# How four tiles of the first layernorm are turned, and how every turned tile is moved, in a hybrid attention block

## The chip, the cores and the metric

The kernel runs on one core of one Trainium2 chip. The metric is the device time of one execution in microseconds; it is given as the median of several runs. One execution is also recorded by the hardware profiler; its span and its rows are what the text calls the profile and the trace.

## The reference, cut to what matters

The input x is 2 x 1024 x 512 in fp32. Four blocks follow each other, each on the layernorm of the running x, and each added to it.

```python
x = x + attn_a(layernorm(x), ...)   # chunks of 128: gated linear attention with decay
x = x + ffn(layernorm(x), ...)      # silu(x Wg) * (x Wu), then Wd; integer weights, hidden 1408
x = x + attn_b(layernorm(x), ...)   # softmax attention over 1024 positions, output weights
x = x + ffn(layernorm(x), ...)      # the same ffn again

def layernorm(x, eps=1e-5):
    m = mean(x, -1); v = var(x, -1)
    return (x - m) / sqrt(v + eps)

# attn_a, for one chunk of 128 tokens and one head of 128:
# q, k, v = projections (k normalised); alpha = sigmoid, beta = softplus of projections
# cla = cumsum(log(alpha + 1e-6)); decay = exp(cla_i - cla_j), causal
# y = (q k^T * beta * decay) v + (q state) * exp(cla)
# state = state * exp(cla_end) + v^T (k * beta * exp(cla_end - cla))
```

Every projection contracts over the 512 features. TensorE contracts over partitions, so a normed tile, which has tokens on partitions, must be turned until it has features on partitions.

## The kernel before, in words

**Tiles and groups.** The 2048 tokens are 16 tiles of 128; four tiles are a group (`ST = 4`). The normed x of a group, turned, is called xT (128 partitions by 4 x 512). The four norms are named a (input of attn_a), f (first ffn), b (attn_b) and g (second ffn); x1, x2 and x3 are the running x after the first, second and third block, kept in DRAM as 16 tiles each.

**Precision.** Products that need fp32 are made of three fp32r products (`mm3`, L89 to L91): each operand is split into a high part (ScalarE cast, L75) and a low part (subtraction on VectorE, L76).

**Two ways of turning.** For the first two groups of norm a (tiles 0 to 7), `ln_tile` normalises a tile on VectorE (xn, L122) and `layernorm_T` transposes its four 128 x 128 pieces on TensorE (L130) into PSUM, from which the split is made. All other groups, 14 in number, go through `ln_steps`: four norm steps (`ln_norm`: load x at L102, statistics at L109 and L111, three small GpSimd operations, xn, then one VectorE transpose of 32 x 32 blocks into the tile y, L198) and four moves (`ln_move`, L209: four transfers each, from 32 partitions of y to 32 partitions of xT, with the blocks of 32 tokens interleaved, so that one piece is 32 values or 128 bytes). `ln_split` then splits xT.

**Order.** An ordered list of Python calls says what each engine does next, and a scheduler orders instructions by it. `behind(...)` adds edges: what is written in it comes after the given instructions. In attn_a, the start is: the product M of two weights, tiles 0 to 3, gate projections, then for each head i `q_head(0, i)`, with tiles 4 to 7 between them, then the loads and splits of Wk and Wv (`load_wqkv`, `load_wv`), the keys and values of tile 0 (`kv_tile(0)`), and a loop over the 16 tiles. In turn t of the loop stand the query projections of head t of the next group (`q_head`), the keys and values of tile t + 1, the scores of tile t, and the steps in `fill[t]`, which hold norm steps of later groups. `spill` writes M to DRAM: `m_d`, L181 and L183.

**Queues.** The loads of x and weights, the stores and most xT transfers are issued in order by SyncE (SP). Some xT transfers of norms b and g go by GpSimd.

**The late operand step.** In the second half of attn_b, `combine("g", 0)` prepares the second ffn's operands from xT in a list of steps called `moving`. `do(moving, n)` runs the next n. One of them, T1, is a subtraction (L257), a ScalarE cast and a VectorE subtraction of 128 x 1024.

The names that the text uses: pWk and pWv are the products for keys and values, pq those for queries, pS the scores' product, pob the output product of attn_b with ptl and pth the split probabilities; `lu` and `la` are the logs of the gates, for which ScalarE loads a function table.

Of the kernel before, what the change touches and what calls it, by code (L numbers as in the profile page):

```python
# [9 lines left out]
F32 = mybir.dt.float32  # L10
# [6 lines left out]
P = 128  # L17
# [8 lines left out]
ST = 4  # L26
# [8 lines left out]
def hybrid_block_kernel(ctx: ExitStack, tc: tile.TileContext, a, out):  # L35
# [30 lines left out]
    def behind(inss):  # L66

        es = ExitStack()
        for ins in inss:
            es.enter_context(tc.issue_after(ins))  # L70
        return es
# [28 lines left out]
    def load_x(src, name, tag="xin"):  # L100
        xin = (rp if tag == "xres" else xp).tile([P, D], F32, tag=tag, name=f"xin_{name}")
        nc.sync.dma_start(out=xin, in_=src)  # L102
        return xin
# [31 lines left out]

    bq_s, sg_s, su_s = cols[:, 0:H], cols[:, H : H + KH], cols[:, H + KH : H + 2 * KH]

    x_in = a["x"]
    x1 = [dp.tile([P, D], F32, tag=f"x1_{t}", name=f"x1_{t}") for t in range(NT)]
    x2 = [dp.tile([P, D], F32, tag=f"x2_{t}", name=f"x2_{t}") for t in range(NT)]  # L140
    x3 = [dp.tile([P, D], F32, tag=f"x3_{t}", name=f"x3_{t}") for t in range(NT)]
    cl_d = [dp.tile([16, P], F32, tag=f"cl_{g}", name=f"cl_{g}") for g in range(NST)]
    p_d = [dp.tile([T // P, P, P], F32, tag=f"p_{i}", name=f"p_{i}") for i in range(NC)]
    vo_d = [dp.tile([P, 1024], F32, tag=f"vo_{k}", name=f"vo_{k}") for k in range(KD)]
# [43 lines left out]
    def ln_norm(src, nm, st, i):  # L188


        t = st * ST + i
        for n in range(t, min(t + 2, st * ST + ST)):
            if (nm, n) not in lnX:
                lnX[nm, n] = load_x(src[n], f"{nm}{n}")
        if i == 0:
            lnY[nm, st] = yp.tile([P, 4, KD, ST, 32], F32, tag="y", name=f"y_{nm}{st}")
        xn = layernorm(lnX[nm, t], f"{nm}{t}", by_act=nm in "af")
        done = nc.vector.transpose(lnY[nm, st][:, :, :, i, :], xn.rearrange("p (k b q) -> p b k q", k=KD, b=4))  # L198
        laid[:] = [done.ins]

    def ln_move(nm, st, b):

        if b == 0:
            lnT[nm, st] = slot(f"xT_{nm}{st}").rearrange("p (k c) -> p k c", k=KD)
        y = lnY[nm, st]
        xf = lnT[nm, st].bitcast(F32).rearrange("p k (i b q) -> p (k i) b q", i=ST, b=4)
        for c in range(4):
            sync = nm in "af" or (nm, st) in (("b", 0), ("b", 1), ("g", 3)) or ((nm, st) == ("b", 2) and c % 2)
            (nc.sync if sync else nc.gpsimd).dma_start(  # L209
                out=xf[32 * b : 32 * (b + 1), :, c, :],  # L210
                in_=y[32 * c : 32 * (c + 1), b].rearrange("p k i q -> p (k i) q"),
            )

    def ln_split(nm, st):
# [133 lines left out]
    with ExitStack() as actx:  # L348
# [41 lines left out]
        def load_wv():  # L390
            wv = slot("Wv")
            wqkv["Wv"] = [wv[:, k * 512 : (k + 1) * 512] for k in range(KD)]
            for k in range(KD):
                w = wqkv["Wv"][k]
                stg = sp.tile([P, 512], F32, tag="stg", name=f"stg_Wv{k}")
                nc.sync.dma_start(out=stg[:, 0:256], in_=a["Wv"][k * P : (k + 1) * P, 0:256])
                with behind(normed_x):
                    split(w[:, 0:256], w[:, 256:512], stg[:, 0:256], nc.gpsimd if k % 2 else None)

        def load_wqkv(nm, staged=None):  # L400
# [8 lines left out]
                    done.extend(split(w[:, 0:512], w[:, 512:1024], staged[:, k]))  # L409
            return load if staged is None else done  # L410

        xa = [x_in[t * P : (t + 1) * P, :] for t in range(NT)]

        def ln_tile(t):
            st, i = divmod(t, ST)
# [4 lines left out]

        def sm(shape, nm, st, dt=F32):
            return a3.tile([P] + shape, dt, tag=nm, name=f"{nm}_{st}")

        vbs = []

# [151 lines left out]
        def kv_tile(t):  # L577
            kv_part(t, "Wk")
            kv_part(t, "Wv")
# [133 lines left out]
        with behind((end,)):  # L713
            gate_proj(0)
        load_wqkv("Wq", staged)
        for i in range(4):
            ends.clear()
            q_head(0, i)
            with behind((wq_loaded, *ends.values())):
                for t in ((), (4,), (5,), (6, 7))[i]:  # L720
                    ln_tile(t)
            if i == 0:
                load_wqkv("Wk")
            if i == 1:
                with behind((*normed_x, *copied)):
                    spill(ap, ("kT", "kw", "sdec", "at"), pm, m_d, "M")
        load_wv()
        kv_tile(0)
        decays(0)
        k_norm(0)  # L730

        fill = [[] for _ in range(NT)]
        for src, nm, g, its in (
            (xa, "a", 2, (0, 0, 0, 1, 1, 1, 1, 1)),
            (xa, "a", 3, (2, 2, 3, 4, 4, 5, 5, 5)),
            (x1, "f", 0, (6, 6, 7, 7, 7, 7, 8, 8)),
            (x1, "f", 1, (9, 9, 10, 10, 10, 10, 11, 11)),
        ):
            for t, step in zip(its, ln_steps(src, nm, g)):
                fill[t].append(step)  # L740

        def a_split(g):
            for step in ln_split("a", g):
                step()
            xTa[g] = lnT["a", g]

        moving = combine("f", 0)
        wcs, loads = [], []
        for t in range(NT):
            if t + 4 < NT:  # L750
                q_head(*divmod(t + 4, ST))
            if t == 0:
                decay_rows(0)
                load_row(0)
                load_row(1)
            load_row(t + 1)
            if t + 1 < NT:
                kv_tile(t + 1)
            weighed = scores(t)
            if t % ST == 0 and t + ST < NT:  # L760
                gate_proj(t // ST + 1)
            if t + 1 < NT:
                with behind((*(normed[t + 1][2:] or normed[t][2:]), *key_copy)):
                    decay(t + 1)
            if t == NT - 2:
                with behind(key_copy):
                    for n in (1, 2):
                        loads.append(product_operands(sp, a["WvT"], a["Wo"], "V", n))
                with behind(parts[-4:]):
                    late_norm.pop()()  # L770
            if t in (3, 7):
                with behind(key_copy):
                    a_split(t // 4 + 2)
            with behind(normed.get(t + 1, (weighed,))):
                for step in fill[t]:
                    step()
                if 1 <= t <= KH:
                    down_weights(sp, t - 1)
                for n in {NT - 3: (0,), NT - 1: (3,)}.get(t, ()):
                    loads.append(product_operands(sp, a["WvT"], a["Wo"], "V", n))  # L780
                if t == NT - 3:
                    first_codes = [
                        load_codes(xp, "xn", a["wgu"][0][:, n * 512 : (n + 1) * 512], f"cf0_{n}") for n in range(2)
                    ]
                if t == NT - 2:
                    wcs.append(stationary(0, "f0", loaded=first_codes))

                    room = staging("codes").bitcast(I32)
                    for j in (2, 3):
                        held[j] = [room[:, 2 * j - 4 + n] for n in range(2)]  # L790
                        for n in range(2):
                            nc.sync.dma_start(out=held[j][n], in_=a["wgu"][j][:, n * 512 : (n + 1) * 512])
                for n in range(3 if NT - 4 <= t < NT - 1 else 0):
                    moving.pop(0)()
                if t == NT - 1:
                    wcs.append(stationary(1, "f0", (sp, "stg")))
            if (t + 2) % ST:
                load_row(t + 2)
            if t == NT - 2:
                prep = weight_product(loads, "V")  # L800
            if t >= NT - 2:
                next(prep)
# [5 lines left out]
    def ffn(src, dst, nm, wcs, moving, ended, after):  # L808
# [3 lines left out]
        with ExitStack() as fctx:  # L812
# [5 lines left out]
            for pr in range(2):  # L818
# [90 lines left out]
                for i in range(2 * ST):  # L909
# [4 lines left out]
                            done = h_split(n, js, ha[:, n - 2, js] if n < ST else hb[:, n - ST, js], None)  # L914
                    xr = rp.tile([P, D], F32, tag="xres", name=f"xr{nm}{t}")
                    with behind((half,)):
                        nc.sync.dma_start(out=xr, in_=src[t])
                    o = fp.tile([P, 512], F32, tag="sg", name=f"o{nm}{t}")

                    last = nm == "g" and t == NT - 1  # L920
# [17 lines left out]

    of_b = combine("b", 0)
    ffn(  # L940
        x1,
        x2,
        "f",
        wcs,
        moving,
        spilled,
        (ln_steps(x2, "b", 0) + ln_steps(x2, "b", 1), of_b[:6]),
    )


# [2 lines left out]
    with ExitStack() as bctx:  # L953
# [209 lines left out]
        def do(steps, n):  # L1163
            with behind(last):
                for _ in range(n):
                    steps.pop(0)()
# [32 lines left out]
        wvo = blocks(vo_d, "wvo0_")  # L1199
        moving = of_b[6:]  # L1200
        for b in range(NB):
            nm, src, g = ("b", x2, 2) if b == 0 else ("g", x3, 0)
            norm = ln_steps(src, nm, g) + ln_steps(src, nm, g + 1)
            if b == 0:
                for kt in (4, 5, 6, 7):
# [49 lines left out]
            def between():  # L1255
                out_b(b, 3)
                if b:
                    with behind(summed):
                        do(moving, 2)

            cycle(b, 3, between)
            if b == 0:
# [5 lines left out]
        probs_T(1, 7)  # L1268
        probs_split(1, 7, last)
        with behind(splits):  # L1270
            do(moving, 6)
        array(out_b, 1, 5)
        array(out_b, 1, 6)
        wcs = [stationary(n, "g0") for n in range(2)]
        ended = (array(out_b, 1, 7),)

    out_t = [out[t * P : (t + 1) * P, :] for t in range(NT)]
    ffn(x3, out_t, "g", wcs, moving, ended, ([], []))


# [60 lines left out]
```

## Time and profile before

| | us |
|---|---|
| median of 3 runs | 927.32 |
| lowest and highest | 926.01, 927.61 |
| the profiled execution's own time | 926.9 |
| span of its trace | 925.2 |
| TensorE busy | 918.5 |
| VectorE busy | 690.4 |
| ScalarE busy | 433.9 |
| GpSimd busy | 257.4 |

The profiled execution's own time is 1.7 us above its span, which runs from the first to the last recorded instruction. TensorE was granted its full clock on average (1.0). Busy times overlap, so they aren't added up: what counts is which engine is on the chain that ended last, and what that engine waited for. A row of a transfer gives its count, its size and the median time from issue to landing; an engine's row gives the count, and the duration of one.

### The profile page before, as it was taken

The numbers are of one execution on the slowest core, as the hardware profiler recorded it, in microseconds if no ns is written. First come the engines' busy times: TensorE is split into PE (matmuls) and PEld (weight loads), VectorE is DVE, ScalarE is ACT, GpSimd is POOL, SyncE is SP. The second block draws the span as 40 slices with busy tenths as digits, with TensorE's granted clock in tenths as the row PEclk, the third lists the DMA queues.
The fourth block names the chain that finished last, engine by engine and source line by source line (L and its number), as shares of the span: only waits on it lengthen the run. The fifth ranks groups of instructions, "written<-read, shape, count | busy, mean of one in ns | idle before, by whom it ended". The sixth has DMA issues, their size and how long they took to land.

```text
span 925.2 us, 13659 instructions
## 1 busy us (share of the span) xinstructions
PE 918.5 (99%) x4546; PEld 778.1 (84%) x4546; DVE 690.4 (75%) x1335; ACT 433.9 (47%) x928; POOL 257.4 (28%) x458
## 2 busy tenths in 40 slices
PE   9999999999999999999999999999999999999998
PEld 7899999998888888888888888888878888888887
DVE  6755657479998798778848878569968886967654
ACT  5645365556776334444234444145434444344431
POOL 4345334557563002211130401140501631001100
PEclk9999999999999999999999999999999999999999
DMA  9535655477979754724733769225969735454022
GB/s 304 210 100 124 208 160 152 158 207 262 367 236 321 214 178 153 216 47 150 281 82 83 171 168 261 69 45 137 239 140 369 259 126 137 165 205 138 22 69 80
DMA packets 216182, 162.20 MB, mean 175 GB/s; under 512 B 151024, under 2 KB 167728, under 8 KB 216112
## 3 DMA queue, kind: packets, MB, share of 16 engines
q1 hardware_dynamic: 212624, 150.05, 53.7%
q0 software_dynamic: 3488, 11.28, 4.5%
q8 instruction: 36, 0.59, 0.3%
q14 instruction: 34, 0.28, 0.1%
HBM read 104.76 MB, written 41.84 MB: 158 GB/s over the span
## 4 chain that ended last, share of the span: by engine, by line
PE 94%; DVE 2%; SPq 1%; DMA 1%; issue 1%; ACT 0%; POOL 0%; DVEq 0%; ACTq 0%
PE pXf L338 4%; PE pog L925 4%; PE pog L924 4%; PE pZf L338 4%; PE pof L925 4%; PE pXg L338 4%; PE pVg L338 4%; PE pVf L338 4%; PE pZg L338 4%; PE pof L924 4%; PE pob L91 3%; PE pob L89 3%; PE pob L90 3%; PE psZ L1023 2%; PE psX L1023 2%; PE psV L1023 2%
## 5 line engine op out<-in xcount | busy, mean ns | idle before, releaser
L924 PE MATMUL pog<-wdg,hsg 128*128 128x512 f32 (+1 forms) x165 | 60.1, 375 | 0.0
L925 PE MATMUL pog<-wdg,hsg 128*128 128x512 f32 (+1 forms) x165 | 60.0, 375 | 0.0
L925 PE MATMUL pof<-wdf,hsf 128*128 128x512 f32 x154 | 59.1, 389 | 0.0
L924 PE MATMUL pof<-wdf,hsf 128*128 128x512 f32 x154 | 58.9, 389 | 0.0
L91 PE MATMUL pob<-vh,ptl 128*128 128x512 f32 x128 | 49.9, 390 | 0.8 <-DVE ptl L76 0.8
L89 PE MATMUL pob<-vh,pth 128*128 128x512 f32 x128 | 49.9, 390 | 0.0
L90 PE MATMUL pob<-vl,pth 128*128 128x512 f32 x128 | 49.8, 389 | 0.0
L76 POOL TENSOR_TENSOR hsg<-sgg,hsg 128x128 fp32r<-128x128 f32 x40 | 18.9, 491 | 110.4 <-ACT hsg L75 102.6
L338 PE MATMUL pXg<-B_g,wcg 128*128 128x512 f32 x176 | 46.2, 389 | 0.0
L338 PE MATMUL pVf<-T_f,wcf 128*128 128x512 f32 x176 | 46.2, 389 | 0.0
L338 PE MATMUL pVg<-T_g,wcg 128*128 128x512 f32 x176 | 46.2, 389 | 0.0
L338 PE MATMUL pXf<-B_f,wcf 128*128 128x512 f32 x176 | 45.9, 390 | 0.0
L113 POOL TENSOR_SCALAR ve_g<-mv_g 128x1 f32<-128x1 f32 x16 | 7.7, 486 | 129.6 <-DVE mv_g L111 129.6
L209 POOL DMA_DIRECT2D xT_g<-y_g x48 | 31.1, 655 | 38.5 <-DVE T_b L76 29.2
L338 PEld LDWEIGHTS pXf<-B_f,wcf 128*128 128x128 f32 x176 | 32.9, 188 | 7.1 <-issue 0.3
L338 PEld LDWEIGHTS pVf<-T_f,wcf 128*128 128x128 f32 x176 | 33.0, 188 | 6.9
L338 PEld LDWEIGHTS pVg<-T_g,wcg 128*128 128x128 f32 x176 | 33.0, 188 | 6.9
L338 PEld LDWEIGHTS pXg<-B_g,wcg 128*128 128x128 f32 x176 | 33.0, 188 | 6.9
L545 ACT ACTIVATE row<-row,ncl 128x128 f32<-128x128 f32 x64 | 20.5, 391 | 35.4 <-POOL row L534 35.4
L113 POOL TENSOR_SCALAR ve_b<-mv_b 128x1 f32<-128x1 f32 x16 | 5.7, 359 | 112.4 <-DVE mv_b L111 112.2
L924 PEld LDWEIGHTS pog<-wdg,hsg 128*128 128x128 f32 x165 | 31.1, 188 | 5.7
L925 PEld LDWEIGHTS pog<-wdg,hsg 128*128 128x128 f32 x165 | 31.0, 188 | 5.6
(344 smaller groups left out, 2837.4 us busy)
## 6 DMA issues: line engine op xcount, KB each, us to landing
wcg<-wc SPq DMA_DIRECT2D x19, 896.0 KB, 5.0
wc<-wcf SPq DMA_DIRECT2D x11, 896.0 KB, 5.8
p<-py SPq DMA_DIRECT2D x15, 512.0 KB, 3.5
wcf<-wc SPq DMA_DIRECT2D x8, 896.0 KB, 6.3
ptl<-p SPq DMA_DIRECT2D x56, 128.0 KB, 3.1
xin_a<-in_x SPq DMA_DIRECT2D x16, 256.0 KB, 5.3
xra<-in_x SPq DMA_DIRECT2D x16, 256.0 KB, 3.4
row<-cl SPq DMA_DIRECT2D x16, 256.0 KB, 4.3
```

The source lines that it names most:

```text
L76: return c.ins, (eng or nc.vector).tensor_tensor(lo, src, hi.bitcast(F32), ALU.subtract).ins
L89: nc.tensor.matmul(ps, lhs_hi, rhs_hi, start=first, stop=False)
L90: nc.tensor.matmul(ps, lhs_hi, rhs_lo, start=False, stop=False)
L91: end = nc.tensor.matmul(ps, lhs_lo, rhs_hi, start=False, stop=last).ins
L113: nc.gpsimd.tensor_scalar(ve, mv[:, 1:2], EPS, None, ALU.add)
L209: (nc.sync if sync else nc.gpsimd).dma_start(out=xf[32 * b : 32 * (b + 1), :, c, :], in_=y[32 * c : 32 * (c + 1), b].rearrange("p k i q -> ...
L338: nc.tensor.matmul(ps, w[:, m, k * P : (k + 1) * P], o[:, s, k, :], start=first and k == 0 and s == 0, stop=k == 1 and s == 1, skip_group_ ...
L545: nc.scalar.activation(row[:, h, :], row[:, h, :], AF.Exp, bias=ncl[:, n : n + 1], scale=-1.0)
L924: nc.tensor.matmul(ps, hs[i][0][:, j], wd[j][:, ds], start=j == 0, stop=False)
L925: nc.tensor.matmul(ps, hs[i][1][:, j], wd[j][:, ds], start=False, stop=j == KH - 1)
L1023: ends[nm] = nc.tensor.matmul(ps, o[:, i, k], w[:, j, k], start=first and k == 0 and i + j == 0, stop=k == 1 and i == 1, skip_group_check= ...
```

## The change: what it does

1. Tiles 4 to 7 of norm a no longer go through `ln_tile`. They are a group of `ln_steps`, like groups 2 and 3: xn by ScalarE, transposes by VectorE, 16 transfers by SyncE, then `a_split(1)`.
2. Every `ln_move` transfer now has pieces of 128 values (512 bytes) in place of 32. For this, tile i of a group takes rows c * 128 + i * 32 + q of the group (c and i from 0 to 3, q from 0 to 31), so the load of a tile is four blocks of 32 rows. x1, x2 and x3 are one DRAM tile for each group, of 512 rows, in place of four.
3. The four loads of group 1 are issued at its first step, two into the buffers of another pool.
4. `kv_tile(1)` stands ahead of the first query head of group 1, whose products come behind it.
5. The spill of M and the splits of Wv come behind `laid` (the last VectorE transpose of a norm) in place of `normed_x`.
6. In the last cycle of attn_b, one step of `moving` in place of two is run between the score products, and seven in place of six behind the last split of probabilities.

```diff
+    def in_tiles(groups):
+        return [x[i * P : (i + 1) * P, :] for x in groups for i in range(ST)]
-    x1 = [dp.tile([P, D], F32, tag=f"x1_{t}", name=f"x1_{t}") for t in range(NT)]
+    x1_g = [dp.tile([ST * P, D], F32, tag=f"x1_{g}", name=f"x1_{g}") for g in range(NST)]
+    x1 = in_tiles(x1_g)
...
-        for n in range(t, min(t + 2, st * ST + ST)):
+        first = (nm, st) == ("a", 1)
+        for n in range(t, min(t + (4 if first else 2), st * ST + ST)):
             if (nm, n) not in lnX:
-                lnX[nm, n] = load_x(src[n], f"{nm}{n}")
+                rows = src[st].rearrange("(c i q) d -> i c q d", c=4, i=ST)
+                tag = "xres" if first and n % ST > 1 else "xin"
+                lnX[nm, n] = load_x(rows[n - st * ST], f"{nm}{n}", tag)
...
-        xf = lnT[nm, st].bitcast(F32).rearrange("p k (i b q) -> p (k i) b q", i=ST, b=4)
+        xf = lnT[nm, st].bitcast(F32)
...
-                out=xf[32 * b : 32 * (b + 1), :, c, :],
-                in_=y[32 * c : 32 * (c + 1), b].rearrange("p k i q -> p (k i) q"),
+                out=xf[32 * b : 32 * (b + 1), :, c * P : (c + 1) * P],
+                in_=y[32 * c : 32 * (c + 1), b].rearrange("p k i q -> p k (i q)"),
...
-                with behind(normed_x):
+                with behind(laid):
                     split(w[:, 0:256], w[:, 256:512], stg[:, 0:256], nc.gpsimd if k % 2 else None)
...
+        norm1 = ln_steps(x_g, "a", 1)
         for i in range(4):
             ends.clear()
             q_head(0, i)
             with behind((wq_loaded, *ends.values())):
-                for t in ((), (4,), (5,), (6, 7))[i]:
-                    ln_tile(t)
+                for step in ((), norm1[:4], norm1[4:], ())[i]:
+                    step()
...
-                with behind((*normed_x, *copied)):
+                with behind((*laid, *copied)):
                     spill(ap, ("kT", "kw", "sdec", "at"), pm, m_d, "M")
         load_wv()
+        a_split(1)
         kv_tile(0)
...
         for t in range(NT):
+            if t == 0:
+                ends.clear()
+                kv_tile(1)
             if t + 4 < NT:
-                q_head(*divmod(t + 4, ST))
+                with behind(ends.values() if t == 0 else ()):
+                    q_head(*divmod(t + 4, ST))
...
-            if t + 1 < NT:
+            if 0 < t < NT - 1:
                 kv_tile(t + 1)
...
                     with behind(summed):
-                        do(moving, 2)
+                        do(moving, 1)
...
         with behind(splits):
-            do(moving, 6)
+            do(moving, 7)
```

More of the change, by code (lines that the diff above doesn't have):

```diff
@@ L136, in hybrid_block_kernel @@
     bq_s, sg_s, su_s = cols[:, 0:H], cols[:, H : H + KH], cols[:, H + KH : H + 2 * KH]
+    def in_tiles(groups):
+        return [x[i * P : (i + 1) * P, :] for x in groups for i in range(ST)]
     x_in = a["x"]
-    x1 = [dp.tile([P, D], F32, tag=f"x1_{t}", name=f"x1_{t}") for t in range(NT)]
-    x2 = [dp.tile([P, D], F32, tag=f"x2_{t}", name=f"x2_{t}") for t in range(NT)]
-    x3 = [dp.tile([P, D], F32, tag=f"x3_{t}", name=f"x3_{t}") for t in range(NT)]
+    x1_g = [dp.tile([ST * P, D], F32, tag=f"x1_{g}", name=f"x1_{g}") for g in range(NST)]
+    x1 = in_tiles(x1_g)
+    x2_g = [dp.tile([ST * P, D], F32, tag=f"x2_{g}", name=f"x2_{g}") for g in range(NST)]
+    x2 = in_tiles(x2_g)
+    x3_g = [dp.tile([ST * P, D], F32, tag=f"x3_{g}", name=f"x3_{g}") for g in range(NST)]
+    x3 = in_tiles(x3_g)
     cl_d = [dp.tile([16, P], F32, tag=f"cl_{g}", name=f"cl_{g}") for g in range(NST)]
@@ L410, in load_wqkv @@
             return load if staged is None else done
-        xa = [x_in[t * P : (t + 1) * P, :] for t in range(NT)]
+        x_g = [x_in[g * ST * P : (g + 1) * ST * P, :] for g in range(NST)]
+        xa = in_tiles(x_g)
         def ln_tile(t):
@@ L422, in sm, with a_split @@
             return a3.tile([P] + shape, dt, tag=nm, name=f"{nm}_{st}")
+        def a_split(g):
+            for step in ln_split("a", g):
+                step()
+            xTa[g] = lnT["a", g]
         vbs = []
@@ L719, in hybrid_block_kernel @@
             with behind((wq_loaded, *ends.values())):
-                for t in ((), (4,), (5,), (6, 7))[i]:
-                    ln_tile(t)
+                for step in ((), norm1[:4], norm1[4:], ())[i]:
+                    step()
             if i == 0:
@@ L733, in hybrid_block_kernel @@
         for src, nm, g, its in (
[L734 to L737, printed above, removed]
+            (x_g, "a", 2, (0, 0, 0, 1, 1, 1, 1, 1)),
+            (x_g, "a", 3, (2, 2, 3, 4, 4, 5, 5, 5)),
+            (x1_g, "f", 0, (6, 6, 7, 7, 7, 7, 8, 8)),
+            (x1_g, "f", 1, (9, 9, 10, 10, 10, 10, 11, 11)),
         ):
@@ L740, in hybrid_block_kernel @@
                 fill[t].append(step)
[L742 to L745, printed above, removed]
         moving = combine("f", 0)
@@ L916, in ffn @@
                     with behind((half,)):
-                        nc.sync.dma_start(out=xr, in_=src[t])
+                        nc.sync.dma_start(out=xr, in_=in_tiles(src)[t])
                     o = fp.tile([P, 512], F32, tag="sg", name=f"o{nm}{t}")
@@ L940, in hybrid_block_kernel @@
     ffn(
-        x1,
+        x1_g,
         x2,
@@ L946, in hybrid_block_kernel @@
         spilled,
-        (ln_steps(x2, "b", 0) + ln_steps(x2, "b", 1), of_b[:6]),
+        (ln_steps(x2_g, "b", 0) + ln_steps(x2_g, "b", 1), of_b[:6]),
     )
@@ L1201, in hybrid_block_kernel @@
         for b in range(NB):
-            nm, src, g = ("b", x2, 2) if b == 0 else ("g", x3, 0)
+            nm, src, g = ("b", x2_g, 2) if b == 0 else ("g", x3_g, 0)
             norm = ln_steps(src, nm, g) + ln_steps(src, nm, g + 1)
@@ L1277, in hybrid_block_kernel @@
     out_t = [out[t * P : (t + 1) * P, :] for t in range(NT)]
-    ffn(x3, out_t, "g", wcs, moving, ended, ([], []))
+    ffn(x3_g, out_t, "g", wcs, moving, ended, ([], []))
 def _layouts(i):
```

## The prediction

> **What bounds the kernel now.** I read the page from the top, then the waits of the bound engine, then the timeline of the two places that the change touches. The page first: busy shares, TensorE's granted clock, the packets, the chain that ended last, and four rows of transfers (size, median microseconds from issue to landing).
>
> ```profile
> span 925.2 us, 13659 instructions
> PE 918.5 (99%) x4546; PEld 778.1 (84%) x4546; DVE 690.4 (75%) x1335; ACT 433.9 (47%) x928; POOL 257.4 (28%) x458
> PEclk9999999999999999999999999999999999999999
> DMA packets 216182, 162.20 MB, mean 175 GB/s; under 512 B 151024, under 2 KB 167728, under 8 KB 216112
> PE 94%; DVE 2%; SPq 1%; DMA 1%; issue 1%; ACT 0%; POOL 0%; DVEq 0%; ACTq 0%
> ...
> xin_a<-in_x SPq DMA_DIRECT2D x16, 256.0 KB, 5.3
> out<-xrg SPq DMA_DIRECT2D x15, 256.0 KB, 2.0
> xT_a<-y_a SPq DMA_DIRECT2D x32, 64.0 KB, 2.1
> ```
>
> TensorE is the bound: 99% busy, 94% of the chain. So a change gains only what it takes off TensorE's own list or out of its waits, and loses whatever new wait it gives TensorE. The waits of TensorE in the whole run are these (total, times, longest):
>
> ```profile
> PE warm L685 <- POOL ones L356: 1.3, 1, 1.3
> PE pob L91 <- DVE ptl L76: 0.8, 1, 0.8
> PE pxT_a L130 <- DVE xn_a L122: 0.5, 1, 0.5
> PE pS L650 <- ACT kT L624: 0.4, 1, 0.4
> ```
>
> None is a wait for a transfer: the 128-byte pieces cost TensorE nothing now. The timeline (start, duration) shows SyncE's issues around tiles 4 to 7, one xT group, ScalarE's table load, the cold start, and the late operand step:
>
> ```profile
> 15.15 3.16 SPq L102 DMA_DIRECT2D xin_a<-in_x  x4
> 18.74 0.97 SPq L82 DMA_DIRECT2D stg_Wk<-in_Wk  x2
> ...
> 75.42 11.91 SPq L209 DMA_DIRECT2D xT_a<-y_a  x16
> ...
> 38.10 1.28 ACT L465 ACT_TABLE_LOAD   x1
> ...
> 1.26 3.78 PE L685 MATMUL warm<-ones 128*128 128x128 f32 x16 [1.26 <-POOL ones L356]
> ...
> 680.48 1.05 ACT L75 CAST T_g<-xT_g 128x1024 fp32r<-128x1024 f32 x1 [0.22 <-DVE xT_g L257]
> 681.44 0.68 ACT L1073 ACTIVATE pe<-psV,nm 128x512 f32<-128x512 f32 x1
> 681.57 1.23 DVE L76 TENSOR_TENSOR T_g<-xT_g,T_g 128x1024 fp32r<-128x1024 f32 x1 [0.73 <-ACT T_g L75]
> ```
>
> **Removed.** Sixteen transposes (L130) leave TensorE between 30.3 and 37.5 us: 16 x 0.109 us start to start = 1.7. Three changes of matmul kind, fp32 to fp32r, go with them at 0.088 each: 0.3. Together -2.0.
>
> **The late operand step.** The cast (1.05) and the subtraction (1.23) stood ahead of the last two exponentials and the split of ptl. Start to start, TensorE lost 0.97 us at 684.4 waiting for ptl. Moved behind that split, they are needed by the pXg products at about 703, some 4 us after they end, so nothing is late in their place: -1.0. The other wait in reach, pS at 99.9 for kT, cost 0.56 start to start; with other work on ScalarE there I count it gone: -0.6. All gains: -3.6. No other edit takes anything off TensorE.
>
> **Pieces of 512 bytes.** An xT transfer of 512 pieces keeps SyncE 0.67 us, transfers of 128 pieces 0.475 apart when back to back (0.375 alone). That is 16 x 0.2 = 3.2 us of SyncE for a group, and 15 groups have it. TensorE waits for none of them, so I price it at 0; the work hiding it is the group of tiles ahead. The price for tiles 4 to 7 is the next step.
>
> **Tiles 4 to 7 on the new path.** This group had no transfers; now it has 16 on SyncE, behind the normed tile's DVE transpose (0.64 each; ScalarE makes xn, 0.81 each, DVE loses 0.52 each). Queued with them on SyncE are the four M_1 stores, in order: two xT transfers stand ahead of or between these, 14 behind. The stores wait for DVE's subtractions, which wait behind `lu`, and that for the table load of 1.28; in before's times the last store is issued at 39.4. Then 39.9 + 13 x 0.475 = 46.1 for the last of the 14, + 1.85 landing + 0.6 for the cast = 48.5. Counting TensorE's instructions in the new order at their spacings, the first value product (pWv) falls at 38.8 and the first query product of tile 4 at 44.8. The wait is 3.7. Tile 1's keys and values ahead of these queries (12 x 0.227 + 12 x 0.12 = 4.2 us of TensorE) are the cover; without that move the wait would be 4.2 longer. Moving the Wv split and the M spill behind `laid` adds no instruction and is priced at 0; the cost if that fails is inside the wait just given.
>
> **The x loads.** Sixty loads of x are written anew: a tile is now four blocks of 32 rows, so the source's outermost count is 4, where each transfer of before has a multiple of 16 on both sides. Bytes and packets stay: 128 packets of 2 KB, 84 ns each in the trace's packet records. Spread over 16 engines that is 0.67 us, as now; over one, 10.75 us. Nothing in the trace shows an outermost count of 4. Between ends so far apart I take four engines, 32 x 0.084 = 2.69 us: the count of the blocks, and the geometric middle of the ends. Each load then delays all that is queued behind it on those engines by 2.0 us, and a lone one lands after 4.0 instead of 2.0.
>
> A rule speaks to this. The Trainium skill, "DMA: Bandwidth & Descriptors", section "Why a DMA increments its semaphore by 16 and not by 1", says that a transfer runs on the largest number of engines up to 16 that divides the outermost dimensions of both patterns. By it these loads run on 4 engines and the forecast below stands; by the row of today's loads it is the first rival. No run here shows it yet.
>
> With 2.69 us: Wq's last part lands at 20.6, then x4, x5, x6 at 23.3, 26.0, 28.7, two Wk parts at 30.0, x7 at 32.7, the other Wk parts at 34.0. ScalarE, in order, casts them and then norms tile 5: 34.0 + 0.5 + 0.6 + 0.8 = 36.0 (rounded). That frees x5's buffer for x9 of the next group, which lands at 36.0 + 4.0 = 40.0. Its statistics (0.67) stand on DVE ahead of tile 6's transpose and of `u`: 41.5. Behind `u` on ScalarE are the table load 1.28, lu and la 0.3, a qT 0.6 and the Wv cast 0.5: 44.2. So pWv starts at 44.3 instead of 38.8: +5.5. The M_1 stores follow at about 45.5, 14 xT transfers from 46.0, landing and cast as above: 55.1; TensorE reaches the queries at 44.3 + 6.0 = 50.4: +4.7 (in place of 3.7). Groups 2 and 3 load x in two pairs issued together (0.7 apart) and two single ones. The second of such a pair lands 3.6 later, its statistics ahead of the next tile's gates on DVE; as pS waits for kT already now, I leave 0.5 of slack: 3.1 for each pair, 0.6 for each single: +7.4. The 48 loads of f, b and g have longer cover; ends 0 and 3, taken 1.5. That includes the new wait of a group's first load for the fourth x tile's store (2.3 median), behind which other loads queue on SyncE.
>
> **Sum.** Against the profiled execution's 926.9 (span 925.2; the median of the runs is 927.32): -3.6 + 5.5 + 4.7 + 7.4 + 1.5 = +15.5: 942.4 us.
>
> **Rivals.** *As now:* the loads still use 16 engines. Then only the wait of 3.7 is new: -3.6 + 3.7 = +0.1, 927.0, with -1.6 to +2.4 for xT spacings of 0.375 to 0.475 and a hiccup of the queue like the 1.7 us that one xT issue took. For it: bytes and packets are the same. Against it: the pattern differs from each one shown.
>
> *Faster:* SyncE runs the 16 xT transfers early enough. Its place is the first query product of tile 4; it decides when the last xT piece lands by about 45, 3 us sooner than I have it, which needs the M_1 stores out of the way and 0.375 apart (14 x 0.1 = 1.4, the stores 1.6). Then at most 0.7 of wait is left: -2.9, 924.0. Against it: the stores' wait for the table load is in the trace.
>
> *Longer wait:* loads as now, but the wait of 3.7 is long enough to lower TensorE's speed. The row: the 16 warming passes at the start took 3.78 us, 0.22 each on average, later 0.112. Sixteen such slow passes cost 1.7; with a hiccup of 0.9, 0.1 + 2.6 = +2.7: 929.6. The Trainium skill, "TensorE: Matmul & The Clock Gate", Part 1, states that an idle window of about 3.4 us halves the clock, which would make this likely; no wait in this trace is longer than 1.3, so the clock after one isn't shown.
>
> **Chances.** Four engines 0.58, as now 0.20, faster 0.10, longer wait 0.10, one engine (far above the range) 0.02. Four gets over half because the block count is the one property in which these loads differ from every row. About 0.2% (1.9 us) can be told from no change. As now gives 0.16 same, 0.02 each side. So faster 0.12, same 0.16, slower 0.72. The range goes from 926, which takes in most of as now, to 950: four engines with f, b and g at 3, both long waits followed by slow passes (2 x 1.7) and hiccups (about 2). The likeliest case alone: 934 to 950.
>
> **What would show it.** TensorE's waits: pWv for Wv, pq for xh_a near 50, pS for kT near 77 and 103; an xin row with landings some 2 us or more longer. Right in part: L130 for tiles 4 to 7 gone, no pob wait at 684, xT issues near 0.4. If xin lands as before, with one wait of 3 to 4 us near 45, it is *as now*; with no wait at all there, *faster*. A clock below full after 45 us speaks for *longer wait*. If the loads are slow but DVE's statistics don't delay ScalarE, my chains are wrong.

## The result and the profile after

The changed kernel takes 1009.22 us (median of 4 runs, 1008.87 to 1013.93) where the kernel before takes 927.47 beside it: a ratio of 1.0896 (95% interval 1.0862 to 1.093), 81.75 us slower. The forecast was slower, 942.4 us, with a range up to 950. The direction and the likeliest case (loads of x on four engines) were right. The size was short by a factor of five, because most of the loss arose where the prediction had put 1.5 us.

From the page of the changed kernel (span, busy time, granted clock in tenths by slice, packets, the chain that ended last and its lines):

```profile
span 1007.6 us, 13664 instructions
PE 945.0 (94%) x4530; PEld 790.3 (78%) x4530; DVE 692.7 (69%) x1335; ACT 437.5 (43%) x932; POOL 247.1 (25%) x462
PEclk9879999999999999999998999999999999999999
DMA packets 159398, 163.24 MB, mean 162 GB/s; under 512 B 72736, under 2 KB 110944, under 8 KB 159328
PE 55%; DMA 24%; DVE 6%; POOL 5%; issue 3%; ACT 3%; SPq 3%; DVEq 0%; POOLq 0%; ACTq 0%
DMA xin_f<-x 6%; DMA xin_a<-in_x 5%; PE pog L943 4%; PE pog L942 4%; PE pVg L349 3%; PE pof L943 3%; PE pof L942 3%; PE pZg L349 3%; PE pXg L349 3%; PE pZf L349 3%; PE pXf L349 3%; DMA xin_b<-x 3%; PE pVf L349 3%; PE psZ L1041 2%; DMA xin_g<-x 2%
```

TensorE fell from 94% of the chain to 55%; a quarter of the chain is now transfers, and those named are all loads of x: xin_f, xin_a, xin_b, xin_g. TensorE has 16 instructions fewer and yet is busy 26.5 us longer, so its passes became slower; the clock row says where (slices 2, 3 and 22). TensorE's waits, the eight with the largest totals (total, times, longest):

```profile
PE pS L667 <- ACT kT L641: 11.0, 7, 3.2
PE pq L89 <- ACT xh_a L75: 10.1, 3, 7.3
PE psY L1041 <- ACT opS L75: 8.2, 1, 8.2
PE pd L652 <- POOL kw L629: 4.5, 4, 2.1
PE pWv L89 <- ACT Wv L75: 4.5, 1, 4.5
PE pob L91 <- DVE ptl L76: 4.1, 1, 4.1
PE pVf L349 <- DVE upf L899: 2.9, 1, 2.9
PE pZg L349 <- DVE pZg L897: 2.6, 2, 2.4
```

They stand in every stage (pS, pq, pd and pWv in attn_a, pVf in the first ffn, psY and pob in attn_b, pZg in the second ffn), not only where tiles 4 to 7 are turned. Measured start to start, that is from the start of one pass to the start of the next against the spacing of such a pair in the kernel before, TensorE lost 63.4 us in waits (before: 2.4) and 26.1 in passes slower than their spacing of before (before: 2.8); it saved 2.0 on transposes. 61.0 + 23.3 - 2.0 = 82.3, the difference of the two spans (82.4).

The row that leads back to the cause is VectorE's waits, first in the changed kernel:

```profile
DVE bn_f L109 <- DMA xin_f<-x: 37.8, 14, 6.6
DVE bn_a L109 <- DMA xin_a<-in_x: 28.5, 11, 4.8
DVE bn_g L109 <- DMA xin_g<-x: 23.3, 10, 5.3
DVE y_b L209 <- DMA xT_b<-y_b: 10.8, 1, 10.8
DVE bn_b L109 <- DMA xin_b<-x: 10.4, 5, 3.1
```

and the same rows of the kernel before, which the prediction did not read:

```profile
DVE bn_f L109 <- DMA xin_f<-x: 14.5, 9, 3.4
DVE bn_a L109 <- DMA xin_a<-in_x: 3.6, 4, 1.6
DVE bn_g L109 <- DMA xin_g<-x: 1.2, 1, 1.2
DVE bn_b L109 <- DMA xin_b<-x: 0.8, 1, 0.8
```

VectorE stood waiting for x 20.1 us in all before, and 100.0 after. In f its statistics had no room to spare even before: 9 of 16 waited. In such a wait VectorE runs nothing else, so the low parts and evictions listed behind it come later, and TensorE waits for those.

That the loads run on four engines is in the packets. The counts fit if each engine that takes part in a transfer adds one semaphore packet of 4 bytes. The kernel before has 10,993 of them for 687 transfers, 16 each and one over; the changed kernel has 703 transfers, and 703 x 16 - 60 x 12 + 1 = 10,529 is just what its trace holds.

### The profile page after: what moved, and what is told of

Same layout as the page of the kernel before. It is cut to its first block, busy times and chain, and to the rows that moved or that the text cites. A ratio compares the mean times of both kernels' runs of the same rounds, so it can differ in the third digit from the quotient of the medians.

```text
span 1007.6 us, 13664 instructions
## 1 busy us (share of the span) xinstructions
PE 945.0 (94%) x4530; PEld 790.3 (78%) x4530; DVE 692.7 (69%) x1335; ACT 437.5 (43%) x932; POOL 247.1 (25%) x462
## 4 chain that ended last, share of the span: by engine, by line
PE 55%; DMA 24%; DVE 6%; POOL 5%; issue 3%; ACT 3%; SPq 3%; DVEq 0%; POOLq 0%; ACTq 0%
DMA xin_f<-x 6%; DMA xin_a<-in_x 5%; PE pog L943 4%; PE pog L942 4%; PE pVg L349 3%; PE pof L943 3%; PE pof L942 3%; PE pZg L349 3%; PE pXg L349 3%; PE pZf L349 3%; PE pXf L349 3%; DMA xin_b<-x 3%; PE pVf L349 3%; PE psZ L1041 2%; DMA xin_g<-x 2%
## 5 line engine op out<-in xcount | busy, mean ns | idle before, releaser
L91 PE MATMUL pob<-vh,ptl 128*128 128x512 f32 x128 | 51.2, 400 | 4.1 <-DVE ptl L76 4.1
L349 PE MATMUL pVg<-T_g,wcg 128*128 128x512 f32 x176 | 47.6, 398 | 0.2 <-DVE upg L899 0.2
L109 DVE BATCH_NORM_STATS2 bn_f<-xin_f 128x6 f32<-128x512 f32 x16 | 11.0, 693 | 37.8 <-DMA xin_f<-x 37.8
L220 POOL DMA_DIRECT2D xT_g<-y_g x48 | 26.3, 555 | 43.3 <-DVE T_b L76 28.3
L89 PE MATMUL pq<-xh_a,Wq 128*128 128x512 f32 x64 | 26.7, 418 | 10.1 <-ACT xh_a L75 10.1
L113 POOL TENSOR_SCALAR ve_b<-mv_b 128x1 f32<-128x1 f32 x16 | 3.5, 228 | 132.9 <-DVE mv_b L111 132.8
```

What stands on the lines that cost most here:

```text
L89: nc.tensor.matmul(ps, lhs_hi, rhs_hi, start=first, stop=False)
L91: end = nc.tensor.matmul(ps, lhs_lo, rhs_hi, start=False, stop=last).ins
L109: nc.vector.bn_stats(bn, xin)
L113: nc.gpsimd.tensor_scalar(ve, mv[:, 1:2], EPS, None, ALU.add)
L220: (nc.sync if sync else nc.gpsimd).dma_start(out=xf[32 * b : 32 * (b + 1), :, c * P : (c + 1) * P], in_=y[32 * c : 32 * (c + 1), b].rearra ...
L349: nc.tensor.matmul(ps, w[:, m, k * P : (k + 1) * P], o[:, s, k, :], start=first and k == 0 and s == 0, stop=k == 1 and s == 1, skip_group_ ...
```

## The experiments

Times are medians, and each difference is to the kernel before in the same series, with the ratio and its interval.

**The number of engines alone.** Three kernels differ from the kernel before only in how a norm step's load names its 128 rows. The tokens of a tile come out permuted and nothing puts them back in order; the work is the same.

```diff
-                lnX[nm, n] = load_x(src[n], f"{nm}{n}")
+                lnX[nm, n] = load_x(src[n].rearrange("(q c) d -> c q d", c=4), f"{nm}{n}")   # c = 4, 8, 16
```

Four blocks:

> The kernel before, but each load of x by a norm step (56 of them, groups 2 and 3 of norm a and all of f, b, g) reads its tile's 128 rows as 4 interleaved blocks, so its source's outermost count is 4; the tokens of a tile are thereby permuted within the norm. Bytes, pieces, buffers and everything else are as before. Theory one, these loads run on 4 engines and their lateness is what costs: 56 x 12 = 672 fewer semaphore packets of 4 bytes than before (10,321 in place of 10,993), and a time of 975 to 1000. Theory two, the new order, the group dependence and the new path of tiles 4 to 7 cost most: the time stays under 945.

Eight:

> As the kernel with 4 blocks, but with 8 blocks of 16 rows (tokens permuted within a tile as well). Theory one: 8 engines, 1.34 us of transfer in place of 0.67, 56 x 8 = 448 fewer semaphore packets (10,545), and a time of 930 to 950, far less than half of what 4 blocks add, since part of the delay fits in the slack. Theory two: as before, within 2 us of 927.

Sixteen, the control:

> As the kernels with 4 and 8 interleaved blocks, with 16 blocks of 8 rows (tokens permuted within a tile): the same kind of pattern, but an outermost count of 16. Theory one (the count sets the engines): the time of before within 2 us, and its 10,993 semaphore packets. Rival (the pattern of three dimensions or the scattered rows cost by themselves): at least 5 us above before.

| blocks | time | above before | ratio | packets |
|---|---|---|---|---|
| none (before) | 927.11 | | | 216182 |
| 16 | 929.33 | 2.4 | 1.0021 (1.0011 to 1.0031) | 216182 |
| 8 | 937.75 | 10.6 | 1.0111 (1.0090 to 1.0132) | 215734 |
| 4 | 981.04 | 53.9 | 1.0578 (1.0547 to 1.0608) | 215510 |

The missing packets are 448 and 672, all of 4 bytes: 56 x 8 and 56 x 12, as theory one has it. With 16 blocks none is missing, and the time is 2.4 us above before: a little more than the 2 allowed, so the scattered rows cost something by themselves, but they are not the cause. The kernels with 4 and 8 blocks ran only twice each (978.56 and 983.52; 936.62 and 938.89). The page and VectorE's waits of the kernel with four blocks:

```profile
DMA packets 215510, 162.19 MB, mean 165 GB/s; under 512 B 150352, under 2 KB 167056, under 8 KB 215440
```

```profile
DVE bn_f L109 <- DMA xin_f<-x: 42.7, 14, 5.0
...
DVE bn_a L109 <- DMA xin_a<-in_x: 19.1, 8, 4.6
DVE bn_g L109 <- DMA xin_g<-x: 15.1, 7, 5.3
```

Nothing else of the change is in that kernel, and VectorE waits 85 us for x. In its packet records the four loads that stand alone take 3.2 to 3.7 us from the first packet to the end of the last; five of six such loads of the kernel before take 1.2 to 1.4. Theory one holds; theory two, under 945, falls. The cost is not in proportion: by the packets' 84 ns, 8 engines add 0.67 us to a load and 4 engines 2.0, three times the delay; the kernels lose 10.6 and 53.9 us, five times as much. Start to start, TensorE loses 6.6 us more than before in waits and 3.2 in slow passes with 8 blocks, 39.9 and 16.8 with 4. So the first part of a delay still fits into what slack there is, and the passes behind the longer waits are slower too.

**Which of the loads.** One condition more, `src[n] if nm == "a" else` ahead of the gather, leaves norm a's 8 loads alone.

> As the kernel with 4 interleaved blocks (981.0), but the 8 loads of norm a keep their rows: 48 loads of f, b and g have an outermost count of 4 (tokens permuted within a tile for these norms), 10,417 semaphore packets. The prediction's step (these loads have longer cover, 1.5 us): at most 931. Theory from the traces (VectorE already waits for x loads in the kernel before, in order, so each later load passes on to TensorE): 955 to 972, most of the loss.

970.47, 43.1 above before (1.0469, 1.0432 to 1.0505). The 48 loads of f, b and g carry four fifths of it; the 8 of norm a the other 10.6. With two runs of each kernel, up to 5 us apart, the split is good to some 3 us. This is the step of the prediction that failed most.

**The changed kernel with its loads on 16 engines.** Either cut in four, with the gathered rows that the 512-byte moves need, or whole, with 128 adjacent rows; the second leaves the tokens of a group permuted in xT.

```diff
-        nc.sync.dma_start(out=xin, in_=src)
+        for c in range(4):                      # kernel 1: gathered tiles only
+            nc.sync.dma_start(out=xin[32 * c : 32 * (c + 1), :], in_=src[c])
...
-                rows = src[st].rearrange("(c i q) d -> i c q d", c=4, i=ST)
+                rows = src[st].rearrange("(i p) d -> i p d", i=ST)        # kernel 2
```

> The changed kernel, but each gathered tile is loaded by four transfers of 32 rows each, so that the outermost count is 32 on both sides. Theory one: all loads run on 16 engines again, the waits of the loop over tiles and of f, b and g go, what stays is one wait for the turned group 1 of 4 to 6 us: 928 to 936. Theory two: the time stays above 960.

> The changed kernel, but each tile's load takes 128 adjacent rows in one transfer, as before (the tokens of a group are then permuted in xT). No load runs on 4 engines and none is cut in four. Theory one, what is left of the loss is the path of tiles 4 to 7 (two waits of 3 and 8 us and slow passes behind them): 936 to 943. Theory two, it is the 180 more issues of the loads cut in four: at most 931.

Cut in four: 945.27 (1.0177, 1.0152 to 1.0202), 64 less than the changed kernel, but 18 above before; neither theory's number. Whole: 933.28 (1.0066, 1.0050 to 1.0081), 6.2 above before, a little under what theory one gave. So 76 of the changed kernel's 82 us go with the gathered loads, and cutting them in four gives back 64 of these: 12 stay, though 16 engines are used (its trace has 16 packets of 4 bytes for each transfer, and one over). TensorE's waits in it are 7.7 for the turned group, 3.1 each at pWv and at pZg of the last block, and small ones. Two things can be behind the 12, and they were not separated. One is the 180 more issues on SyncE. The other is the order of stores and loads: a gathered tile has rows of all four tiles of its group, so it can't be loaded whole until the group's fourth store has landed. SyncE's timelines show it for group 1 of norm f (its first loads, and the fourth store of x1), before and in the changed kernel:

```profile
146.68 1.02 SPq L102 DMA_DIRECT2D xin_f<-x  x2
...
155.05 0.56 SPq L680 DMA_DIRECT2D x<-xra  x1
```

```profile
186.51 0.54 SPq L697 DMA_DIRECT2D x<-xra  x1
...
194.45 1.17 SPq L102 DMA_DIRECT2D xin_f<-x  x2
```

In nine of the twelve groups of f, b and g the kernel before issues the first load 8 to 33 us before the fourth store has landed; so does the changed kernel with whole loads (8 to 34 us). In the changed kernel every first load is issued behind that store.

**Tiles 4 to 7 by themselves.** The changed kernel with whole loads and the old 128-byte pieces keeps the new path of these tiles and the late step:

> The changed kernel with the loads of 128 adjacent rows and with the 128-byte pieces of before: of the change there remain tiles 4 to 7 on VectorE and transfers, their early loads, the order and the late step. Result as the reference. Theory one: 937 to 945, 0 to 2 above the kernel with 512-byte pieces and whole loads, as an xT issue costs 0.63 in place of 0.60. Theory two: at most 932.

935.58 (1.0085, 1.0067 to 1.0103), 8.5 above before: under the 937 of theory one, well above the 932 of theory two. Its longest wait of TensorE and the clock around the main one (start:end, length, TensorE's busy time, granted clock, share and GB/s of the transfers):

```profile
PE pq L89 <- ACT xh_a L75: 8.3, 1, 8.3
```

```profile
44.00:48.00 4.00, 0.74 (x7) 0.96 0.58 100
48.00:52.00 4.00, 0.00 (x0) 0.50 0.57 98
52.00:56.00 4.00, 2.98 (x13) 0.50 0.23 68
56.00:60.00 4.00, 4.00 (x19) 0.76 0.64 196
60.00:64.00 4.00, 4.00 (x33) 1.00 0.15 50
```

Behind the wait of 8.3 us TensorE runs at half its clock until 58. The path saves 2.0 us of transposes and costs 8.3 and the slow passes. SyncE's timeline in the kernel with whole loads and 512-byte pieces shows what the wait is made of:

```profile
36.90 2.56 SPq L189 DMA_DIRECT2D m<-M  x4
39.52 9.76 SPq L220 DMA_DIRECT2D xT_a<-y_a  x14
```

Fourteen transfers in 9.76 us: 0.64 to 0.72 apart and once 1.35, 0.70 on average. They stand where the prediction put them (39.5 for 39.9), but it had them 0.475 apart.

> The kernel with tiles 4 to 7 on the new path, 128-byte pieces and whole loads (935.6), but half of group 1's 16 xT transfers and the low halves of M's stores are issued by GpSimd. Theory: the wait of 8.3 us at the first query product of tile 4 is SyncE's issuing of 14 transfers at 0.7; with 8 on each queue it falls to 2 to 4, its slow passes with it: 928 to 931. Rival: the wait is set by the transposes and stores ahead, and stays above 6: at least 933.

```diff
-            sync = nm in "af" or ...
+            sync = nm in "af" and ((nm, st) != ("a", 1) or c % 2 == 0) or ...
-            low = nc.gpsimd if name == "V" else nc.sync
+            low = nc.gpsimd
```

932.68 (1.0059, 1.0041 to 1.0077). The wait for xh_a fell from 8.3 to 1.4, so it was SyncE's issuing, as the theory says; the time fell by only 2.9, missed 931 and stayed just under the rival's 933. What is late next is in its waits:

```profile
PE pS L667 <- ACT kT L641: 2.0, 3, 1.4
PE pWv L90 <- POOL Wv L76: 1.5, 1, 1.5
PE pq L89 <- ACT xh_a L75: 1.4, 1, 1.4
```

GpSimd's part of the Wv split now stands behind its own eight issues (5.4 us) and a store of M.

**Tiles 4 to 7 back on TensorE, with the gathered rows.** The first kernel loads them cut in four, the second in pairs of tiles, 32 partitions by 2 x 512, into one buffer:

> The changed kernel with loads cut in four transfers of 32 rows, and with tiles 4 to 7 turned by TensorE as before. Theory one: the waits for Wv and for xh_a before 60 us go, and the time is 927 to 934. Theory two: at least 938.

> As the kernel with pieces and whole loads, but with the right rows: two gathered tiles are loaded by four transfers of 32 partitions by 2 x 512, into one buffer of two tiles. Outermost count 32, so 16 engines, and two issues for a tile. Result as the reference. Theory: 56 more issues than whole loads at 0.4 us, mostly in SyncE's idle time, and a buffer freed later: 927 to 932, between whole loads and loads cut in four (935.4). Rival: issues don't matter, 926.5.

935.42 (1.0074, 1.0049 to 1.0099) and 935.52 (1.0085, 1.0071 to 1.0099). The early waits for Wv and xh_a went in the first, as theory one says, but the time missed 934 by little. Its trace has a wait of 5.6 at pZg in the last block; that trace is of the slowest of its four executions (941.2), and two of the others had a mean clock of 1.0, where each wait above 3 us in these traces lowered it, so the wait doesn't explain the median. The second missed as well: it has 56 more transfers than with whole loads, where the first has 168, and takes the same time. So fewer issues brought nothing, which speaks against the theory of the issues. In both a group's first tile is complete only behind the group's fourth store, and VectorE's waits for x are alike, 42.0 and 42.7 us, where whole loads with these pieces have 21.2 (the kernel of pieces alone, below). That this order is the cause is not shown: a pair also frees its buffer for two tiles at once, and no kernel had whole loads that wait for the fourth store. No way of loading the gathered rows was free.

**Pieces alone, and the late step alone.** In the first, tiles are loaded whole (so the tokens are permuted again), the turning of tiles 4 to 7 and the order are as before, and pieces have 512 bytes; the second has only the two numbers of `do(moving, ...)` changed.

> Of the change only the 512-byte pieces, the group tiles and the late step are kept: tiles 4 to 7 on TensorE, tile 1's keys in their old place, whole loads of 128 adjacent rows (the tokens of a group are then permuted in xT). Theory: the pieces cost TensorE nothing and gain nothing, as it waited for none of them: 926.5, the same as with the late step alone, within 1. Rival: the 2.3 us between the two kernels with and without these pieces are a gain of the pieces in themselves: 924 to 925.

> The kernel before with the late operand step alone moved (one step between the score products, seven behind the split). The wait of 0.97 us for ptl goes: 926.4 where before gives 927.4. Rival: the moved split is late at the pXg products or holds the next one, and the time is the same within 0.3 or worse.

925.46 (0.998, 0.9971 to 0.9988) and 926.49 (0.9993, 0.9984 to 1.0001). The late step takes the wait for ptl away, and the time gains 0.6, which its interval can't tell from nothing. With the pieces the gain is 1.5; so the pieces may be worth about 0.9, in kernels of different series. That lies between theory (926.5) and rival (924 to 925). But that kernel leaves the tokens permuted, and each kernel with these pieces and the gathered rows lost 8 us or more. Of all kernels that keep the tokens in order, the late step alone is the only one not slower than before. A design with the permuted order carried through the later stages was not tried.

## Why the prediction was right or wrong

**Four engines: right.** It was the likeliest case, and the semaphore packets show it to the last one. The Trainium skill's rule ("DMA: Bandwidth & Descriptors", section "Why a DMA increments its semaphore by 16 and not by 1"), that the outermost dimensions of both patterns set the number, agrees with these runs: outermost counts of 4, 8 and 16 gave 4, 8 and 16 packets of 4 bytes for each load.

**The chain around group 1: right until 45 us.** Tiles 4, 5 and 6 were to land at 23.3, 26.0, 28.7; VectorE started on them at 22.8, 25.8, 28.8. The +5.5 ahead of and at pWv came to 6.0 (1.0, 0.4 and 4.6 start to start). The next wait, +4.7, came to 7.5 (7.3 in its row): the term mis-sized is "0.475 apart", a spacing of transfers with two-dimensional patterns of 128 pieces, taken for a pattern of three. Counted like the sum before it, with 13 spacings in place of 14, the prediction's own working gives 4.2 here, not 4.7. The changed kernel's xT issues:

```profile
L220 SPq DMA_DIRECT2D xT_a<-y_a x48: 592/599/1836, 44.5 to 153.2; - x48
```

Their median is 0.60 where 512 pieces took 0.63. A quarter of the pieces saves 5% of the issue, and in a row most of them were 0.64 apart where those of before were 0.67, with single ones of 1.4 to 1.9 in both. With whole loads the same term turned the 3.7 of *as now* into 7.1.

**"The 48 loads of f, b and g have longer cover; ends 0 and 3, taken 1.5": wrong, and the largest miss.** Measured: 43.1 with these loads alone on four engines. The upper end was as wrong as the value. The prediction gives no row for either; the one list of waits that it shows is TensorE's, in which no transfer stood. TensorE being busy told nothing of VectorE, whose own list had 14.5 us for xin_f. An engine that already waits for such loads has little cover to give: with these 48 loads on four engines VectorE's waits for x in f, b and g grew by 47.6 us, and the time by 43.1. With one y tile for all groups there was a second link: in attn_b, transposes stood 10.8 us until the moves of the group before had read y, and TensorE waited 8.2 for psY behind it.

The same 1.5 was to hold "the new wait of a group's first load for the fourth x tile's store (2.3 median)". In nine of twelve groups that load had stood 8 to 33 us ahead of the store's landing, and it moved behind it. What this costs stays open. The 56 loads on four engines (53.9) and the change with whole loads (6.2) make 60.1 of the 81.75 us. The other 21.6 may lie in the four gathered loads of group 1, in this order of stores and loads, or in how the parts add up; no run separates them.

**"+7.4" for groups 2 and 3: about right.** 981.04 - 970.47 = 10.6 for these 8 loads, good to some 3 us. That has slow passes in it, which the 7.4 had not, so some of the agreement is luck.

**Slow passes: left out of the sum.** The prediction gave waits of 5.5 and 4.7 and at once had a rival in which a wait of 3.7 slows TensorE, yet the forecast's own sum had no term for it; only its range did (2 x 1.7). They cost 23.3. The Trainium skill's rule ("TensorE: Matmul & The Clock Gate", Part 1) that an idle window of about 3.4 us halves the clock, which the trace of before couldn't show, agrees in part: the clock went to half for 3.4, 6.8 or 10.2 us at a time, but waits of 2.0 to 2.6 us were enough in several places, where the page has about 3.4.

**Removed work: right, and small.** The 16 transposes and three switches are gone, 2.0. The wait for ptl went (in the late step alone); in the changed kernel it came back at another tile as 4.1. The pS wait that I counted gone (-0.6) became 11.0 over seven tiles.

**The rivals.** *As now* falls with the packets. *Faster* falls with the kernel of whole loads: even with 16 engines the xT pieces of group 1 were 7.1 late, not early. *Longer wait* was right in what it says of the clock, as a part of the first case, not in place of it.

## What to carry to other kernels

Read the outermost count of a transfer's two patterns ahead of its bytes: four blocks in the source put loads of x on four engines, where one that stands alone took 3.2 to 3.7 us instead of 1.2 to 1.4, and VectorE waited for them. Price a later load by the waits of the engine that consumes it, not by those of the bound engine; if that engine already waits for the same load, there is little cover (43.1 us lost here for 47.6 more of such waits). And a sum with a wait of more than 2 us in it needs a term for the bound engine's clock.

## What the runs showed of the hardware beyond that

The granted clock falls in steps. In the changed kernel's clock records TensorE is at 0.5 for 3.4, 6.8 or 10.2 us at a time, nine times, 51.2 us in all. It was busy for 39.4 of these; half of that, 20 us, is most of the 23.3 by which its passes were slower. Two of these spells in windows:

```profile
56.00:60.00 4.00, 0.00 (x0) 0.60 0.38 99
60.00:64.00 4.00, 3.08 (x13) 0.50 0.21 68
...
96.00:100.00 4.00, 3.23 (x19) 0.72 0.21 66
```

The second follows a wait of only 2.3 us start to start (2.1 in its row). Start to start, in the changed kernel waits up to 1.9 us left the clock at 1.0 each time; of four between 2.3 and 2.6, three lowered it for 3.4 us. In the kernel with four blocks four waits of 2.0 to 2.1 did so too, but another of 2.0 and one of 2.9 did not; every wait above 3.0 in these two kernels lowered it. So a wait of up to 1.9 us cost nothing beyond itself in these two kernels; between 2.0 and 2.9 it could go either way; and a spell of 3.4 us costs about 1.7 more (half of it, an estimate) where TensorE is busy all through it.

SyncE's time to issue depends little on the number of pieces: 0.60 for 128 pieces of 512 bytes in a pattern of three dimensions, 0.63 for 512 of 128 bytes. GpSimd's fell more, from a mean of 0.655 us to 0.555.
